# A two-layer transformer and state-space block: the scan with all five engines in written order, diagonal matmuls, and its last preparation moved

## The chip, the cores and the metric

The kernel runs on one core of one Trainium2 chip. The metric is the device time of one execution in microseconds (us), as the median of several runs. Engines are named as the profile names them: PE (TensorE matmuls and transposes) with PEld (its weight loads), DVE (VectorE), ACT (ScalarE), POOL (GpSimd) and SP (SyncE, which issues most DMAs). A name with a q, such as SPq or ACTq, is the engine's sequencer. Everything is float32.

## The reference

The input x has 4 sequences of 512 tokens with 512 channels. Layer 0 adds an attention, then a gated feed-forward network (FFN) with weights quantised to three values. Layer 1 adds a selective scan, and then an attention over small latents with a mixture of experts (top 2 of 7 and a shared one). The scan is what matters here:

```python
xz = einsum('btd,rd->btr', x, W_xproj)          # x here is the layer norm, "u"
delta_r, B_mat, C_mat = xz[..., :128], xz[..., 128:144], xz[..., 144:]
delta = softplus(einsum('btr,dr->btd', delta_r, W_dt) + b_dt)
dA = exp(delta[..., None] * -exp(A_log))        # 16 states per channel
Bu = delta[..., None] * B_mat[:, :, None, :] * x[..., None]
h_t = dA_t * h_{t-1} + Bu_t;  y_t = sum over n of h_t * C_t
return y + x * D_param
```

## The kernel before, in words

The four sequences (b = 0 to 3) lie in SBUF as xs[b], tokens on partitions in four tiles t of 128. The stages follow one another: attention of layer 0, FFN, scan, latent attention, router, experts.

**FFN** (lines 594 to 715). For each b, 11 hidden tiles f: `gated` makes 16 matmuls into a pair of PSUM banks (L651, high and low parts of the input, hTh and hTl), ACT takes the silu (L656), DVE the product (L657) and the parts gh and gl, and `down` (L669) adds the tile into four banks one tile later. PE's order is written by hand (`manual_schedule`, L674); the other engines are ordered by a scheduler. Between the matmuls the generator `prepare(b - 1)` (L495) is advanced by `part`: three parts per tile, with some left out at the first two tiles. It makes the inputs of the scan for the sequence whose FFN is done:

- statistics (L107), normalised rows row_s (L122), x += u D on POOL (L508, L509), and uT, the transposed u (L131, L132);
- delta_r as drT (L520, L524), the latents B and C by four matmuls of 512 columns (L529), copied to bcT; C goes to DRAM as c_rows (L536), B is transposed into bts (L540, L543), one column per token tile and state;
- per channel tile k: z by a matmul (L551), |z| on ACT (L552, into the buffer e), max(z, 0) on DVE (L553, into delta); exp(-|z|) on ACT (L555); a correction u = e - ((e + 1) - 1) added to delta by three DVE operations on SBUF (L559 to L561); log(1 + e) (L563) added on DVE (L568). That is the softplus;
- delta to DRAM (L569), delta times u on DVE (L571), transposed (L576), copied (L578) and stored as dxs (L579).

The preparation of b = 3 does not fit behind any FFN tile and runs inside the scan.

**Scan** (lines 815 to 966). The work is 128 steps (b, n, half): 16 states n for each sequence, and two halves of the channel tiles. Only PE is in written order. Before the loop come `fetch(0)` (L894: two loads of 1 MB, delta_l and dxT, L828 and L830) and seven pieces of `prepare(3)` (L900 to L904). At the first half of each state, `scale` of the next state makes on ACT four copies bu of dxT scaled by B (L839) and four exponentials da (L845). In each step PE transposes bu into two banks for the step after (`turn`, L853), DVE runs two scans over time (`scan`, L861), POOL multiplies h by the broadcast C (`weigh`, L872, the load cb at L869 is on SP), and PE adds hc, transposed, into four banks of sums for the step two back (`add_up`, L885; hc has three buffers). After a sequence's last step DVE adds the sums to x (L892). The loads of sequence b + 1 go out at state 3 of sequence b (L912). Further pieces of `prepare(3)` run in odd steps, what is left in step 56 (L923); then pools change hands, and the weights of the latent attention are loaded. From step 76 `enter(0)` (L725), the first preparation of that attention, is advanced in every third step: statistics, normalised h on DVE (L735), squares on ACT (L739), rows on DVE (L749), transposes (L753), latents (L760).

Of the kernel before, what the change touches and what calls it, by code (L numbers as in the profile page):

```python
# [19 lines left out]
P = 128  # L20
# [10 lines left out]
NS = 16  # L31
# [15 lines left out]
def block_kernel(ctx: ExitStack, tc: tile.TileContext, a: dict, out: bass.AP):  # L47
# [46 lines left out]
    dxs = tc.dram_tile([B * T, C], F32, name="dxs")  # L94

# [40 lines left out]
    def project_back(srcT, w, x):  # L136

        for t in range(NT):
            y = bank("y")
            for k in range(NK):  # L140
                nc.tensor.matmul(
                    y, srcT[:, k, t * P : (t + 1) * P], w[:, k, :], start=k == 0, stop=k == NK - 1
                )
            nc.vector.tensor_tensor(x[:, t, :], x[:, t, :], y, ALU.add)

# [337 lines left out]

    def scan_constants(pool):
# [4 lines left out]
        for k in range(NK):  # L489
            diag = pool.tile([P, P], F32, tag="diag", name="diag")  # L490
            nc.vector.tensor_scalar(diag, ident, dcol[:, k : k + 1], None, ALU.mult)
            nc.tensor.matmul(dp[:, k * P : (k + 1) * P], ones, diag, start=True, stop=True)
        nc.scalar.copy(dpar, dp)

    def prepare(b, pool, spot, ahead):  # L495
# [30 lines left out]

        pb = spot("pb")
        for k in range(NK):
            nc.tensor.matmul(  # L529
                pb[: 2 * NS, :], wx[:, k, RANK:], uT[:, k, :], start=k == 0, stop=k == NK - 1  # L530
            )
            if k == 1:
                yield
        bcT = pool.tile([2 * NS, T], F32, tag="bcT", name="bcT")
        nc.scalar.copy(bcT, pb[: 2 * NS, :])
        nc.sync.dma_start(c_rows[b], bcT[NS:, :])  # L536
        yield
        pb = spot("pbt")
        for t in range(NT):
            nc.tensor.transpose(  # L540
                pb[:, t * NS : (t + 1) * NS], bcT[:NS, t * P : (t + 1) * P], ident[:NS, :NS]
            )
        nc.scalar.copy(bts[:, b, :], pb[:, : NT * NS])  # L543
# [45 lines left out]

    def half_pair(name):  # L590
        return pair(name)[:, 0, :]


    with tc.tile_pool(name="b_s", bufs=1) as bs, tc.tile_pool(name="b_1", bufs=1) as b1, tc.tile_pool(
# [16 lines left out]
        def inputs(b, mv=None):  # L611

            high = b2.tile([P, NK, T], F32R, tag="hTh", name="hTh")
            low = b2.tile([P, NK, T], F32R, tag="hTl", name="hTl")
# [59 lines left out]
        with tc.manual_schedule(engines={mybir.EngineType.PE}):  # L674
# [4 lines left out]
            for b in range(B):  # L679
# [14 lines left out]
                for f, rows in enumerate(FROWS):  # L694
# [5 lines left out]
                    part(3 * f + 1)  # L700
                    if b == 0 and f == 4:
                        scan_constants(b2)
# [22 lines left out]
    def enter(b, pool):  # L725

        mv = pool.tile([P, NT, 2], F32, tag="mv", name="mv_d")
        for t in range(NT):
# [3 lines left out]
            yield  # L732
        ss = pool.tile([P, NT], F32, tag="ss", name="ss_d")
        for t in range(NT):
            nc.vector.tensor_scalar(  # L735
                hs[b][:, t, :], xs[b][:, t, :], mv[:, t, 0:1], rs[:, t : t + 1], ALU.subtract, ALU.mult
            )
# [6 lines left out]
        before = None  # L744
        for t in range(NT + 1):
            row = None
            if t < NT:
                row = pool.tile([P, C], F32, tag="row", name="row_d", bufs=2)
                nc.vector.scalar_tensor_tensor(  # L749
                    row, hs[b][:, t, :], rs[:, t : t + 1], ln1, ALU.mult, ALU.mult  # L750
                )
            if before is not None:
# [63 lines left out]
    with tc.tile_pool(name="c_f", bufs=2, reuse_waits="tile") as cf, tc.tile_pool(  # L816
        name="c_1", bufs=1
    ) as c1, tc.tile_pool(name="c_2", bufs=2) as c2:

        das = [c1.tile([P, NK, T], F32, tag=f"da{i}", name=f"da{i}") for i in range(2)]  # L820
        for da in das:
            nc.vector.memset(da[:, :, 0:1], 0.0)
        steps = [(b, n, half) for b in range(B) for n in range(NS) for half in range(2)]
        loaded, scaled, decays, turned, states, weighed, sums = {}, {}, {}, {}, {}, {}, {}

        def fetch(b):
            delta = cf.tile([P, NK, T], F32, tag="delta_l", name="delta_l")
            nc.sync.dma_start(delta, by_rows(deltas[b]))  # L828
            dxT = cf.tile([P, NT, C], F32, tag="dxT", name="dxT")
            nc.sync.dma_start(dxT, by_tokens(dxs, b))  # L830
            loaded[b] = delta, dxT

        def scale(b, n):

            delta, dxT = loaded[b]
            rows = []
            for t in range(NT):
# [10 lines left out]
        def turn(b, n, half):  # L848
            bu = [bank("bu") for _ in range(2)]
            for i in range(2):  # L850
                k = 2 * half + i
                for t in range(NT):
                    nc.tensor.transpose(  # L853
                        bu[i][:, t * P : (t + 1) * P], scaled[b, n][t][:, k * P : (k + 1) * P], ident
                    )
            turned[b, n, half] = bu
# [9 lines left out]
        def weigh(b, n, half):  # L866
# [4 lines left out]
            hc = c2.tile([P, 2, T], F32, tag="hc", name="hc", bufs=3)  # L871
# [5 lines left out]
        def add_up(b, n, half):  # L877
# [12 lines left out]
            if n == NS - 1 and half == 1:  # L890
                for t in range(NT):
                    nc.vector.tensor_tensor(xs[b][:, t, :], xs[b][:, t, :], sums[b][t], ALU.add)  # L892

        fetch(0)  # L894
        last = ExitStack()
        cp = last.enter_context(tc.tile_pool(name="c_p", bufs=1, side="right", reuse_waits="tile"))
        between = prepare(B - 1, cp, bank, 4)
        come = enter(0, c1)
        with tc.manual_schedule(engines={mybir.EngineType.PE}):
            for _ in range(2):  # L900
                next(between)
            scale(0, 0)
            for _ in range(5):
                next(between)  # L904
            turn(*steps[0])
            for m, (b, n, half) in enumerate(steps):
                if half == 0:
# [4 lines left out]
                    if n == 3 and b + 1 < B:  # L912
                        fetch(b + 1)
# [599 lines left out]
```

## Time and profile before

| what | us |
|---|---|
| median of 3 runs (1941.34 to 1942.9) | 1942.84 |
| profiled execution | 1946.77 |
| its span | 1945.0 |
| attention of layer 0 | 0 to 432 |
| FFN | 432 to 753 |
| scan, with the last preparation | 753 to 1122 |
| entry of the latent attention | 1122 to 1157 |
| latent attention | 1157 to 1575 |
| router, experts | 1575 to 1945 |

Busy over the span: PE 1764.7 us (91%), DVE 1145.5, ACT 948.2, POOL 580.9. In the stretch 763 to 1118: PE 286.1, DVE 332.0, ACT 326.6, POOL 311.1 of 355.

How to read the lines below. A group's line gives line, engine, operation, out<-in with partitions x elements, the count, then busy us and mean ns of one, then the engine's idle time just before them and what ended most of it. A line of the timeline gives start and length in us, engine, line, operation, and in brackets the idle time before it with its releaser. A windows line gives the window, its length, then busy us and instruction count of PE, PEld, DVE, ACT and POOL, the granted clock of PE as a share of full speed, the DMA share and GB/s.

### The profile page before, as it was taken

The page shows a single profiled execution, that of the slowest core. Times are in us where ns is not written, and L with a number is a line of the kernel's source. Part 1 is how long each engine was busy: PE and PEld are TensorE (multiplying, and loading weights), DVE is VectorE, ACT ScalarE, POOL GpSimd, SP SyncE. Part 2 cuts the span into 40 slices and gives each one's busy share as a digit, 9 for nine tenths or more (in the row PEclk, how much of TensorE's full clock was granted, in tenths as well). Part 3 has the DMA queues.
Part 4 walks back from the last instruction along what each step waited for, and adds up shares of the span by engine and source line. Part 5 has one row for each costly group of instructions (what it writes and reads, how often), then busy time and mean ns, then how long its engine had stood idle before and what let it go on. Part 6 is the DMA issues. An engine that isn't in the chain of part 4 may idle for free. (4 is left out here: it accounts for less than half of the span.)

```text
span 1945.0 us, 26741 instructions
## 1 busy us (share of the span) xinstructions
PE 1764.7 (91%) x9970; PEld 1060.5 (55%) x9970; DVE 1145.5 (59%) x1849; ACT 948.2 (49%) x1945; POOL 580.9 (30%) x391
## 2 busy tenths in 40 slices
PE   7999999989999897967887889999999988999997
PEld 3433343337666665766776645555555544545443
DVE  6456435666454646999998865564655734322223
ACT  2434433332242436978999836665665732111110
POOL 2221212110202014867998910101000000244430
PEclk9999999999999998989999978999999999999998
DMA  7003200111010104123411100010001006255546
GB/s 245 8 1 99 69 1 1 44 30 47 1 39 7 44 1 152 54 100 89 143 56 46 43 1 1 1 44 1 33 23 38 29 11 235 74 93 91 91 72 190
DMA packets 70884, 114.24 MB, mean 59 GB/s; under 512 B 7962, under 2 KB 26778, under 8 KB 70756
## 3 DMA queue, kind: packets, MB, share of 16 engines
q1 hardware_dynamic: 59796, 88.02, 14.1%
q0 software_dynamic: 8656, 20.32, 5.9%
q10 hardware_dynamic: 2304, 4.20, 0.6%
q8 instruction: 80, 1.31, 0.3%
q14 instruction: 48, 0.39, 0.1%
HBM read 81.18 MB, written 31.33 MB: 58 GB/s over the span
## 5 line engine op out<-in xcount | busy, mean ns | idle before, releaser
L872 POOL TENSOR_TENSOR hc<-h,cb 128x1024 f32<-128x1024 f32 x128 | 303.2, 2410 | 43.3 <-DVE h L861 20.9
L861 DVE TENSOR_TENSOR_SCAN h<-da,bu 128x512 f32<-128x512 f32 x256 | 289.7, 1197 | 15.0 <-ACT da L845 6.9
L853 PE MATMUL bu<-ident,bu 128*128 128x128 f32 x1024 | 165.0, 290 | 55.5 <-DVE h L861 32.7
L271 PE MATMUL pq<-wqkv,hT 128*128 128x512 f32 x384 | 181.2, 620 | 0.7 <-ACT hT L132 0.7
L853 PEld LDWEIGHTS bu<-ident,bu 128*128 128x128 f32 x1024 | 121.7, 147 | 88.6 <-ACT bu L839 49.3
L845 ACT ACTIVATE da<-delta_l,am 128x511 f32<-128x511 f32 x256 | 165.9, 739 | 4.2 <-DVE h L861 4.2
L839 ACT ACTIVATE bu<-dxT,bts 128x512 f32<-128x512 f32 x256 | 165.7, 738 | 0.0
L1101 ACT ACTIVATE pr<-scd,nm 128x128 f32<-128x128 f32 (+3 forms) x256 | 133.1, 528 | 56.3 <-DVE nm L1098 53.6
L651 PE MATMUL pg<-hTh,w 128*128 128x512 f32 (+1 forms) x352 | 148.7, 422 | 9.3 <-DVE sil L657 8.0
L885 PE MATMUL ys<-ident,hc 128*128 128x128 f32 x1024 | 143.4, 285 | 13.4 <-POOL hc L872 11.2
L651 PE MATMUL pg<-hTl,w 128*128 128x512 f32 (+1 forms) x352 | 140.7, 400 | 0.2 <-DVE hTl L639 0.2
L1400 PE MATMUL pgr<-wgu,gTe 128*128 x304 | 137.1, 593 | 0.0
L885 PEld LDWEIGHTS ys<-ident,hc 128*128 128x128 f32 x1024 | 121.6, 147 | 21.7 <-POOL hc L872 18.0
L351 ACT ACTIVATE pt<-sc 128x1024 f32<-128x1024 f32 (+3 forms) x128 | 84.2, 698 | 84.2 <-PE sc L346 81.7
L271 PEld LDWEIGHTS pq<-wqkv,hT 128*128 128x128 f32 x384 | 72.1, 196 | 94.6 <-issue 86.3
L1090 PE MATMUL scd<-qkTd 32*128 32x512 f32 (+3 forms) x512 | 108.3, 504 | 12.9 <-ACT pr L1101 11.9
L102 POOL TENSOR_TENSOR ri_ln<-ri_ln,minus_half 128x4 f32<-128x4 f32 (+1 forms) x17 | 16.9, 994 | 302.6 <-DVE ri_ln L101 298.4
L1098 DVE TENSOR_REDUCE nm<-scd 128x2 f32<-128x256 f32 (+3 forms) x128 | 104.2, 815 | 0.0
L1113 PEld LDWEIGHTS tpd<-ident,pr 128*128 128x128 f32 x640 | 70.4, 145 | 61.0 <-issue 41.5
L1113 PE MATMUL tpd<-ident,pr 128*128 128x128 f32 x640 | 102.2, 292 | 0.6 <-ACT pr L1101 0.6
L352 POOL TENSOR_SCALAR_AFFINE_SELECT pt<-pt 128x512 f32<-128x512 f32 x64 | 43.5, 679 | 196.2 <-ACT pt L351 196.2
L1093 DVE TENSOR_TENSOR scd<-scd,neg 128x256 f32<-128x256 f32 x128 | 54.9, 430 | 69.8 <-PE scd L1090 67.7
(260 smaller groups left out, 3109.1 us busy)
## 6 DMA issues: line engine op xcount, KB each, us to landing
cb<-c_rows SPq DMA_DIRECT2D x64, 256.0 KB, 3.2
q_w<-in_w2T SPq DMA_DIRECT2D x20, 256.0 KB, 2.8
deltas<-delta SPq DMA_DIRECT2D x16, 256.0 KB, 2.1
dxs<-st SPq DMA_DIRECT2D x16, 256.0 KB, 2.5
delta_l<-deltas SPq DMA_DIRECT2D x4, 1024.0 KB, 9.0
dxT<-dxs SPq DMA_DIRECT2D x4, 1024.0 KB, 7.1
acc<-h SPq DMA_DIRECT2D x16, 256.0 KB, 2.0
hrows<-h SPq DMA_DIRECT2D x4, 1024.0 KB, 4.3
```

What stands on the lines that cost most here:

```text
L271: nc.tensor.matmul(y, inputs_T[b][:, k, t * P : (t + 1) * P], wqkv[:, k, s * C : (s + 1) * C], start=k == 0, stop=k == NK - 1,)
L651: nc.tensor.matmul(pg[:rows, i, :], w[:, k, f * P : f * P + rows], part[:, k, :], start=k + m == 0, stop=k + m == NK,)
L839: nc.scalar.activation(row, dxT[:, t, :], AF.Copy, scale=bts[:, b, t * NS + n : t * NS + n + 1])
L845: nc.scalar.activation(da[:, k, 1:], delta[:, k, 1:], AF.Exp, scale=am[:, k, n : n + 1])
L853: nc.tensor.transpose(bu[i][:, t * P : (t + 1) * P], scaled[b, n][t][:, k * P : (k + 1) * P], ident)
L861: nc.vector.tensor_tensor_scan(h[:, i, :], decays[b, n][:, 2 * half + i, :], bu, 0.0, ALU.mult, ALU.add)
L872: nc.gpsimd.tensor_tensor(hc, states.pop((b, n, half)), weighed[b, n].unsqueeze(1).to_broadcast([P, 2, T]), ALU.mult)
L885: nc.tensor.matmul(sums[b][t][:, k * P : (k + 1) * P], hc[:, i, t * P : (t + 1) * P], ident, is_transpose=True, start=n == 0 and k == 0, s ...
L1090: nc.tensor.matmul(sc[:, i, :w], qkT[at, g, t * P : w], qkT[at, NG + g, :w], start=True, stop=True)
L1101: nc.scalar.activation(pr[:, i, :w], sc[:, i, :w], AF.Exp, bias=nm[:, i : i + 1], accum_out=sums[b, g][:, t, 2 * p + i : 2 * p + i + 1],)
L1113: nc.tensor.transpose(tp[:, j * P : (j + 1) * P], pr[:, i, j * P : (j + 1) * P], ident)
L1400: nc.tensor.matmul(pg, gT[:, k, :], wgu[:, bass.ds(e, 1), k, :].rearrange("p e o -> p (e o)"), start=k == 0, stop=k == NK - 1,)
```

## The change

All line numbers in this section are those of before.

- **Order.** In the scan all five engines (PE, DVE, ACT, POOL, SP) run in written order. A step issues: batch-end additions (`finish`, now three steps into the next sequence), a piece of the last preparation, a piece of `enter(0)`, `scale`, the first bank of the next `turn`, the scans, the product, `add_up` of the step three back (hc has four buffers), and the second bank of the next `turn`.
- **Diagonals.** For token tile 0 the scaled copy of dxT and its transposes are replaced by a matmul of dxT with a diagonal matrix of B, which SP loads from DRAM (64 KB per state). ACT makes three copies per state. The diagonals of all 16 states are made when the sequence is prepared: one DVE product of 128x2048, and a store of 1 MB to `diags`, from SP in the FFN and from ACT in the scan. In the FFN the product is written to the buffer e, which |z| overwrites next.
- **Latents.** 16 matmuls of 128 columns, which put the token tiles side by side on the partitions, and one transpose replace four matmuls of 512 columns and four small transposes; C is stored in four parts. The preparation has one piece fewer there.
- **Last preparation** (`prepare_last`). Rows by ACT (scale and shift) in place of DVE; e + 1 and - 1 by ACT; the four terms of the softplus (max(z, 0), e, minus ((e + 1) - 1), logarithm) are summed by PE into a bank, with the identity and its negative as weights; u D is a product with diagonals on PE, added by DVE. Its DMAs go out on ACT. Three pieces come in steps 0 to 2, then one in each odd step from 5, the rest in step 84.
- **Loads.** `fetch(b)` goes out in quarters. The buffers are shared with hTh and hTl of the FFN, so that `fetch(0)` goes out at the start of the FFN's last sequence; those of b = 1 and 2 in four steps of the sequence before, that of b = 3 in steps 84 to 87. The weights of the latent attention are loaded one per step from step 88.
- **`enter`.** Shifted h and rows on ACT instead of DVE, for every b. The weight ln1 is multiplied into the two weight matrices by eight POOL operations in steps 100 to 106, instead of into the rows. The 14 pieces of `enter(0)` run from step 86 to 125.

The diff, cut to its core:

```diff
+    def shift_of(pool, mv, rs):
+        shift = pool.tile([P, NT], F32, tag="shift", name="shift")
+        nc.vector.scalar_tensor_tensor(shift, mv[:, :, 0], -1.0, rs, ALU.mult, ALU.mult)
+        return shift
+
+    def shifted(dst, x, t, rs, shift):
+        nc.scalar.activation(
+            dst, x[:, t, :], AF.Identity, bias=shift[:, t : t + 1], scale=rs[:, t : t + 1]
+        )
...
+    large = scans.enter_context(tc.tile_pool(name="large", bufs=2, reuse_waits="tile"))
+    def fetch(b):
+        delta = large.tile([P, NK, T], F32, tag="one", name="delta_l")
+        dxT = large.tile([P, NT, C], F32, tag="two", name="dxT")
+        loaded[b] = delta, dxT
+        for i in range(NT):
+            nc.sync.dma_start(dxT[:, i, :], by_tokens(dxs, b)[:, i, :])
+            nc.sync.dma_start(delta[:, i, :], by_rows(deltas[b])[:, i, :])
+            yield
...
+    def latents(pb, uT):
+        for k in range(NK):
+            for t in range(NT):
+                nc.tensor.matmul(
+                    pb[t * 2 * NS : (t + 1) * 2 * NS, :P], wx[:, k, RANK:], uT[:, k, t * P : (t + 1) * P],
+                    start=k == 0, stop=k == NK - 1,
+                )
...
+    def keep_inputs(b, pb, room):
+        nc.scalar.copy(
+            bts[:, b, :].rearrange("p (t n) -> p t n", t=NT),
+            pb[:, :P].rearrange("p (t n) -> p t n", t=NT)[:, :, :NS],
+        )
+        diag = room.rearrange("p k t -> p (k t)").rearrange("p (n q) -> p n q", n=NS)
+        nc.vector.tensor_tensor(
+            diag, ident.unsqueeze(1).to_broadcast([P, NS, P]),
+            bts[:, b, :NS].unsqueeze(2).to_broadcast([P, NS, P]), ALU.mult,
+        )
+        return diag
...
     def prepare(b, pool, spot, ahead):
...
+        keep_latents(b, bcT, nc.sync)
         yield
         pb = spot("pbt")
+        nc.tensor.transpose(pb[:, :P], bcT, ident)
+        e = pool.tile([P, NK, T], F32, tag="e", name="diag_s")
+        nc.sync.dma_start(diags[b], keep_inputs(b, pb, e))
         yield
...
+    def prepare_last(b, pool):
...
+        diag = keep_inputs(b, pb, pool.tile([P, NK, T], F32, tag="ln", name="diag_s"))
+        relu = pool.tile([P, NK, T], F32, tag="relu", name="relu")
+        for k in range(NK + 1):
+            if k > 0:
+                nc.scalar.activation(e[:, k - 1, :], pz, AF.Abs, bias=bdt[:, k - 1 : k])
+                nc.vector.tensor_scalar(relu[:, k - 1, :], pz, bdt[:, k - 1 : k], 0.0, ALU.add, ALU.max)
+            if k < NK:
+                pz = bank("pz")
+                nc.tensor.matmul(pz, wdt[:, k * P : (k + 1) * P], drT, start=True, stop=True)
+            if k == NK // 2:
+                nc.scalar.dma_start(diags[b], diag)
+            yield
+        over = pool.tile([P, NK, T], F32, tag="over", name="over")
+        for k in range(NK):
+            nc.scalar.activation(e[:, k, :], e[:, k, :], AF.Exp, scale=-1.0)
+            if k % 2 == 1:
+                yield
+        for k in range(NK):
+            nc.scalar.activation(over[:, k, :], e[:, k, :], AF.Identity, bias=ones[:, 0:1])
+            nc.scalar.activation(over[:, k, :], over[:, k, :], AF.Identity, bias=minus_one)
+            yield
+        ln = pool.tile([P, NK, T], F32, tag="ln", name="ln")
+        nc.scalar.activation(ln, e, AF.Ln, bias=1.0)
+        yield
...
+        terms = ((ident, relu), (ident, e), (minus, over), (ident, ln))
...
+                for i, (w, term) in enumerate(terms):
+                    nc.tensor.matmul(pd, w, term[:, k, :], start=i == 0, stop=i == 3)
...
         def scale(b, n):
             delta, dxT = loaded[b]
-            rows = []
-            for t in range(NT):
+            diag = c1.tile([P, P], F32, tag="diag", name="diag_l", bufs=3)
+            nc.sync.dma_start(diag, diags[b][:, n, :])
+            rows = [diag]
+            for t in range(1, NT):
...
+        def turn(b, n, half, i):
+            bu = bank("bu")
+            k = 2 * half + i
+            nc.tensor.matmul(
+                bu[:, :P], loaded[b][1][:, 0, k * P : (k + 1) * P], scaled[b, n][0],
+                start=True, stop=True,
+            )
+            for t in range(1, NT):
+                nc.tensor.transpose(
+                    bu[:, t * P : (t + 1) * P], scaled[b, n][t][:, k * P : (k + 1) * P], ident
+                )
...
+        engines = {getattr(mybir.EngineType, e) for e in ("PE", "DVE", "Activation", "Pool", "SP")}
+        with tc.manual_schedule(engines=engines):
             scale(0, 0)
-            for _ in range(5):
-                next(between)
-            turn(*steps[0])
+            turn(*steps[0], 0)
+            turn(*steps[0], 1)
             for m, (b, n, half) in enumerate(steps):
+                if m % each == 3 and b > 0:
+                    finish(b - 1)
+                if m >= 5 and m % 2 == 1:
+                    next(between, None)
+                if m >= 86 and m % 3 == 2 and m < 86 + 3 * 14:
+                    next(come)
...
                 if m + 1 < len(steps):
-                    turn(*steps[m + 1])
+                    turn(*steps[m + 1], 0)
                 scan(b, n, half)
                 weigh(b, n, half)
-                if m >= 2:
-                    add_up(*steps[m - 2])
+                if m < 3:
+                    next(between, None)
+                if m >= 3:
+                    add_up(*steps[m - 3])
+                if m + 1 < len(steps):
+                    turn(*steps[m + 1], 1)
-                if m == 56:
+                if m == 84:
...
+            for step in steps[-3:]:
                 add_up(*step)
+            finish(B - 1)
```

## The prediction

> **What bounds the kernel now.** I read the profile page first, then windows by stage, then the scan's own groups, waits and timeline. Two stages are touched, the gated FFN (432 to 753 us from the span's start) and the scan (753 to 1122); the attention before and the stages after 1157 keep their code. The windows show what limits each (columns: window, length, busy us and count of PE, PE weight loads, DVE, ACT, POOL, then the granted PE clock, DMA share, GB/s):
>
> ```profile
> 432.00:753.00 321.00, 304.25 (x1292) 224.58 (x1292) 173.00 (x279) 119.15 (x168) 40.05 (x30) 0.99 0.11 35
> 795.00:870.00 75.00, 55.66 (x375) 47.59 (x374) 74.28 (x68) 70.48 (x108) 54.79 (x24) 0.90 0.25 85
> 955.00:980.00 25.00, 22.00 (x169) 17.93 (x168) 25.00 (x25) 25.00 (x42) 24.66 (x12) 1.00 0.36 128
> ```
>
> The FFN is TensorE's: 304 of 321 us. In the scan's quiet part (955 to 980) DVE, ACT and POOL are all full. While the last preparation runs (795 to 870) DVE is full, ACT nearly, and POOL has fallen to 73%. The groups of the scan:
>
> ```profile
> L872 POOL TENSOR_TENSOR hc<-h,cb 128x1024 f32<-128x1024 f32 x128 | 303.2, 2410 | 43.3 <-DVE h L861 20.9
> L861 DVE TENSOR_TENSOR_SCAN h<-da,bu 128x512 f32<-128x512 f32 x256 | 289.7, 1197 | 15.0 <-ACT da L845 6.9
> ...
> L845 ACT ACTIVATE da<-delta_l,am 128x511 f32<-128x511 f32 x256 | 165.9, 739 | 4.2 <-DVE h L861 4.2
> L839 ACT ACTIVATE bu<-dxT,bts 128x512 f32<-128x512 f32 x256 | 165.7, 738 | 0.0
> ```
>
> In the quiet part the starts of consecutive products on POOL are 2.335 us apart, scans on DVE 1.11 (2.22 a step), exponentials and copies on ACT 0.613, and transposes 0.109, sixteen a step (1.75). Two steps of one state n so cost POOL 4.67, DVE 4.44, ACT 8 x 0.613 = 4.91 and PE 3.5. From the first scan (762.6) to the end of the last product (1117.9) the stage takes 355.3 us; in 763 to 1118 DVE is busy 332.0, ACT 326.6, POOL 311.1. So none is full, and the 7% over the fullest is lost where DVE is held up and the others follow. The timeline shows how: L560 there takes 2.74 us, and a PE wait stands behind it:
>
> ```profile
> 832.97 2.74 DVE L560 TENSOR_TENSOR u<-e,u 128x512 f32<-128x512 f32 x1
> ...
> 837.68 0.72 PEld L853 LDWEIGHTS bu<-ident,bu 128*128 128x128 f32 x4 [4.08 <-ACT bu L839]
> ...
> 841.86 2.74 DVE L561 TENSOR_TENSOR delta<-delta,u 128x512 f32<-128x512 f32 x1
> ```
>
> The same shapes beside an idle POOL took 0.67 to 0.7 us. In this stage L560 averages 1.72 and L568 1.42, and L735 of the next stage's entry reaches 2.59; DVE operations that read PSUM beside the same POOL (L553, L892) stay at 0.66 to 0.75. Steps with such work last 5.4 to 8.8 us in place of 2.3 (steps 21, 23, 25, 31, 47, 49, 101).
>
> **1. The start of the scan.** PE idles 6.31 us (750.94 to 757.65) for DVE's row_s, and the first scan starts at 762.6. The old order puts seven pieces of preparation and both 1 MB loads (issued 752.7 and 753.2) ahead of it. The new one loads batch 0 in quarters during the FFN's last batch, and the first steps need only 3 copies and an exponential: from about 749.3, 3 x 0.61 + 1.28 (table load, L845's row) + 0.61 gives 753; the FFN's last addition on DVE ends at 752.7. First scan about 753.3: **-9.3 us**, bounds -6 (the clock was 0.5 from 752 for 10.24 us, which doubles the first transposes, and the two clears of da go first) and -12.
>
> **2. The scan.** Per state ACT does 3 copies instead of 4, so 7 x 0.613 = 4.29: under POOL's 4.67. The last preparation costs ACT: rows 4 x 0.61, transposes out 4 x 0.49, drT 0.59, bcT 0.25, Abs 4 x 0.69, exponentials 4 x 0.61, eight identities x 0.61, logarithm 1.92 with two table loads of 1.28, eight copies x 0.59, thirteen DMA issues at most x 0.34 (L1451 issues from ACT at 0.338), and the entry of the next stage 10.3: 40 us together. DVE's extras: eight statistics x 0.72, one 128x2048 product 2.29 (L1332's row), relu 4 x 0.66, twelve batch-end additions and four of D u at 0.6, four products with uT x 0.66: 24. POOL: three powers x 1.0 and eight 128x256 scalings x 0.5: 7. Sums: ACT 64 x 4.29 - 4.3 (the last state copies nothing ahead) + 40.2 = 310.5; DVE 128 x 2.22 + 23.9 = 308.3; POOL 128 x 2.335 + 7 = 305.9. PE stays under 2.3 a step. Lower end: the largest sum, 311, if buffers absorb every piece. Upper end: the sum over the 64 states of the dearest engine in each, 345. Today's stage is 1.07 of its fullest engine; 1.07 x 311 = 332, and as the stretched DVE operations that make today's excess leave, and adding up three steps behind with four hc buffers gives PE one step more, I take 330. **-25.3 us** (bounds -44 to -10).
>
> What could replace the removed copy: row 0 of bu now comes from a matmul with a diagonal that SP loads (64 KB per state). cb of 256 KB lands in 3.2 us median and the new load is issued a state ahead (4.67 us), so it costs nothing unless SP's issue is late; uncovered it would hold PE by about 3 us at that state. A diagonal matmul is f32 with 128 columns. The f32 matmuls of L271, 512 columns, start 0.429 us apart at full clock: 0.107 per 128, the same as a transpose, so PE keeps 1.75 a step.
>
> The Trainium skill (FP8 and Floating Point Precision, TensorE Precision Notes) speaks against this part: true FP32 takes four passes through the array. If a transpose were one pass and the matmul four, two of the sixteen would cost 0.33 more each, 2.40 a step, and PE would pass POOL for 8 us more in 128 steps. L271's row does not show that excess over transposes, and I go by the row.
>
> All five engines are now in written order, so a late operand stops what is queued behind it: an ACT piece waiting for a preparation matmul holds the next state's copies and exponentials, and through da the scan. That is in the distance from 311 to 345. After PE gaps of 2.84 us (at 554) and 6.31 us (at 757) the rows show a granted clock of 0.5 in windows of 3.41 and 10.24 us; 16 transposes then take 3.5 a step, over POOL's 2.335. The quiet part ran at 1.00 with almost nothing but transposes, so I put this in the upper end.
>
> **3. The FFN.** Batches 1 to 3 of it prepare scan inputs between matmuls. PE's order is by hand, so what a piece waits for is PE's stall. Removed per piece set: four latents matmuls (1.72) become sixteen small ones (4 x 0.11): -1.3. Added: a 128x2048 product on DVE (2.29) and a 1 MB store from the buffer that Abs writes next. So bts copy, product 2.29, issue 0.4, store, Abs 0.69, relu 0.75, and only then the second pz's pair of banks is free; PE waits there, and behind Abs on ACT stand the silu and the high part of the next FFN tile. A 1 MB store SBUF to DRAM in this kernel (hrows<-h) lands after 4.3 us median. The second pz would then start 5.8 us later than the matmul before it would let it, and an idle window of that length lowers the clock for 3.41 us, +1.7. One piece fewer moves the later pieces up by one part, which shortens a PE wait of 3.1 us there and its half clock (clock 0.5 from 553.98 for 3.41 us) by 3.5. So 5.8 + 1.7 - 1.3 - 3.5 = +2.7 for b = 1, 2, and 4.5 + 1.7 - 1.3 = +4.9 for b = 3, where other parts are used: **+10**. Lower end -7, the store hidden and only the gains left. Upper end +43, if the store takes 15.3 us, as the 1 MB x<-in_x loads do (three times 11 more).
>
> **4. After the scan.** The next stage's entries get 12 to 16 us of ACT for what DVE did. They lie in 1122 to 1157, where ACT is busy 12.6 of 35 us and PE 30.3, and later beside attention, where PE is busy 392 of 418: +2 (bounds -1 to +7). The weight loads spread from step 88 to the end on SP leave ahead of their first use but for the last two; nothing.
>
> Sum: -9.3 - 25.3 + 10 + 2 = -22.6. The profiled execution took 1946.77 us (span 1945.0), 3.9 over the median of the three runs, 1942.84. So 1924.2 profiled, **1920 us** as a median.
>
> **Rivals.** *A, the engines pack:* the stage runs at its largest sum, 312 instead of 330 (-18), and the store hides in part (0 to -12): 1890 to 1908. For it: POOL already runs back to back through 25 steps. Against: 345 of the unbuffered sum. *B, pieces stall the written orders:* 345 (+15) with the FFN as forecast: 1935, to 1939 with a further half-clock window. For it: every piece lands on one state and ACT's logarithm (4.5 us in one) exceeds the buffers' lead of about one state. *C, slower:* the store of the diagonals. PE has no other work ahead of the second pz; at the 15.3 us of the 1 MB loads the FFN gives back 43, not 10: 1953. It decides from a landing of 4.3 + 22.6/3 = 11.8 us. For: the 1 MB loads x<-in_x and wqkv at 15.3 and 10.1 us. Against: those came in the crowded first 60 us, this one meets a DMA share of 0.11. *D, no change:* B and half of C together, 1939 to 1947. That the code does not do what it says is excluded by the instruction order: ACT has 3 copies and 4 exponentials per state, PE 1 matmul and 3 transposes per bank.
>
> **Chances.** Forecast (1908 to 1935) 0.5; A 0.2; B 0.15; D 0.06; C 0.09. 0.2% of 1942.84 is 3.9 us, about what a measurement of this kernel can tell from no change. Faster 0.85, same 0.06, slower 0.09. The range leaves out C, D's upper half and A's lower end: 1895 to 1941.
>
> **What would show it.** Step 1: a first scan between 752 and 756. Step 2: 320 to 340 us from first scan to last product, no DVE operation of the stage over 1.2 us but the product and batch ends, no step over 4.5. Step 3: a PE wait of about 6 us before the second pz of each prepared batch, ended by Abs. Step 4: pl of the first entry 4 us after the last product, as now. I am wrong if products on POOL are over 2.4 us apart in quiet steps, if PE's clock stays under 0.9 in the scan, or if the store's landing is over 8 us.

## The result, and the profile after

The changed kernel takes the same time: 1943.08 us median (1939.54 to 1949.36, 12 runs) against 1942.88 for the kernel before in the same rounds, ratio 1.0003, 95% interval 0.999 to 1.0015. The forecast was 1920. Its profiled execution took 1941.63 us (span 1939.9). Single executions of either kernel differ by up to 10 us, so I compare stages of the profiles, not single times.

| stage, us | before | after | step of the prediction |
|---|---|---|---|
| FFN, first to last matmul | 318.9 | 321.3 | +10 |
| from there to the first scan | 11.3 | 3.0 | -9.3 |
| first scan to the end of the last product | 355.3 | 359.2 | -25.3 |
| from there to the latent attention's first scores | 38.9 | 37.6 | +2 |
| the rest | 788.3 | 785.6 | 0 |

The same windows of the changed kernel (window, length, then busy us of PE, PEld, DVE, ACT, POOL, clock, DMA share, GB/s):

```profile
432.00:753.00 321.00, 294.95 (x1354) 223.11 (x1355) 176.96 (x277) 119.47 (x170) 40.41 (x30) 0.98 0.15 49
795.00:870.00 75.00, 67.98 (x550) 60.58 (x549) 67.71 (x63) 65.55 (x108) 62.81 (x27) 0.98 0.32 101
955.00:980.00 25.00, 24.58 (x174) 19.79 (x173) 21.63 (x20) 21.42 (x36) 20.59 (x9) 1.00 0.37 104
```

In the second window POOL has gone from 54.8 to 62.8 us: the old bad stretch is better. In the third it has gone from 24.7 to 20.6: the stretch that was full is now full of holes. The page's groups of the scan (the copies are 192 instead of 256):

```profile
L1038 POOL TENSOR_TENSOR hc<-h,cb 128x1024 f32<-128x1024 f32 x128 | 300.9, 2387 | 109.3 <-DVE h L1027 90.4
L1027 DVE TENSOR_TENSOR_SCAN h<-da,bu 128x512 f32<-128x512 f32 x256 | 291.4, 1199 | 26.4 <-PE bu L1019 13.3
...
L1007 ACT ACTIVATE da<-delta_l,am 128x511 f32<-128x511 f32 x256 | 163.9, 709 | 6.1 <-DVE h L1027 6.1
...
L1001 ACT ACTIVATE bu<-dxT,bts 128x512 f32<-128x512 f32 x192 | 124.2, 711 | 24.3 <-PE bu L1019 22.5
```

POOL's idle 109.3 contains the wait of 67.9 us ahead of the first product; 41.4 lie inside the scan. ACT now waits 22.5 us for PE: its spare time is not used.

The best reading is by step: the distance between starts of successive products on POOL, less the quiet 2.335 us. The excess of all 128 steps is 57.9 us after and 50.3 before (where, besides, the first product comes 6.1 us after the first scan, now 2.4). In the changed kernel the quiet steps are as forecast (2.31 to 2.35 us in steps 6 to 16, 39 to 52 and 108 to 125); the excess sits in few places:

| steps | excess, us | what stands there |
|---|---|---|
| 85 | 6.5 | diag_l and cb late on SP |
| 84 | 3.7 | the clearing of wr on POOL, which waits for a store to land |
| 34, 66, 98 | 8.1 | batch-end additions on DVE, and a piece |
| 100, 102, 104, 106 | 8.3 | scalings by ln1 on POOL, the second power |
| 17, 30 | 7.1 | instructions that wait at the head of a line; the product of the diagonals |
| 55 | 4.2 | logarithm on ACT with two table loads |
| 0 to 2 | 4.0 | statistics between the first scans |
| 72, 78 | 3.7 | ux, which waits for ACT's copy of delta |
| 94 | 2.4 | 128x4 operation on DVE |
| others | 10.0 | up to 0.7 each, relu, additions of u D, statistics |

The two largest together, steps 84 and 85, in the timeline of the changed kernel (start, length, engine, line, in brackets the idle time and its releaser):

```profile
994.29 0.33 SPq L1106 DMA_DIRECT2D ln<-in_ln_w  x1
...
994.37 0.20 POOL L1109 MEMSET wr<- 128x128 f32 x1 [3.55 <-DMA dxs<-st]
...
997.60 0.43 SPq L997 DMA_DIRECT2D diag_l<-diags  x1
998.08 0.43 SPq L1035 DMA_DIRECT2D cb<-c_rows  x1
...
1002.73 0.77 PE L1014 MATMUL bu<-diag_l,dxT 128*128 128x128 f32 x2 [7.82 <-DMA diag_l<-diags]
...
1003.37 4.67 POOL L1038 TENSOR_TENSOR hc<-h,cb 128x1024 f32<-128x1024 f32 x2 [6.48 <-DMA cb<-c_rows]
```

The load of ln2 and the clearing of wr (the router's weights) take memory of the last preparation, whose store of dxs must land first. POOL stands 3.55 us at the clearing, with a product behind it (step 84). SP is in written order too, so diag_l and cb, which the next steps need, stand behind the load of ln2 and behind four of the eight loads for b = 3 (step 85). At step 30 the same happens on DVE, for 2.83 us and then the 2.29 of the product:

```profile
839.39 0.19 ACT L533 COPY bts<-pbt 128x64 f32<-128x64 f32 x1
839.49 1.95 ACT L1001 ACTIVATE bu<-dxT,bts 128x512 f32<-128x512 f32 x3
839.62 2.29 DVE L538 TENSOR_TENSOR diag_s<-ident,bts 128x2048 f32<-128x2048 f32 x1 [2.83 <-ACT bts L533]
...
844.29 2.37 POOL L1038 TENSOR_TENSOR hc<-h,cb 128x1024 f32<-128x1024 f32 x1 [4.55 <-DVE h L1027]
```

In the FFN the forecast wait is there, for b = 1 and 2:

```profile
538.03 0.69 ACT L603 ACTIVATE e<-pz,bdt 128x512 f32<-128x512 f32 x1 [5.54 <-DMA diags<-diag_s]
538.75 0.75 DVE L604 TENSOR_SCALAR delta<-pz,bdt 128x512 f32<-128x512 f32 x1 [4.11 <-ACT e L603]
539.55 1.22 PE L602 MATMUL pz<-drT,wdt 128*128 128x512 f32 x1 [4.59 <-DVE delta L604]
```

### The profile page after: what moved, and what is told of

It is laid out like the page before. It is cut to its first block, busy times and chain, and to the rows that moved or that the text cites. A ratio compares the mean times of both kernels' runs of the same rounds, so it can differ in the third digit from the quotient of the medians.

```text
span 1939.9 us, 27518 instructions
## 1 busy us (share of the span) xinstructions
PE 1778.6 (92%) x10374; PEld 1096.5 (57%) x10374; DVE 1119.0 (58%) x1812; ACT 938.5 (48%) x1932; POOL 574.7 (30%) x391
## 5 line engine op out<-in xcount | busy, mean ns | idle before, releaser
L1038 POOL TENSOR_TENSOR hc<-h,cb 128x1024 f32<-128x1024 f32 x128 | 300.9, 2387 | 109.3 <-DVE h L1027 90.4
L1019 PE MATMUL bu<-ident,bu 128*128 128x128 f32 x768 | 134.5, 283 | 7.0 <-ACT bu L1001 6.9
L1001 ACT ACTIVATE bu<-dxT,bts 128x512 f32<-128x512 f32 x192 | 124.2, 711 | 24.3 <-PE bu L1019 22.5
L1014 PE MATMUL bu<-diag_l,dxT 128*128 128x128 f32 x512 | 109.0, 296 | 26.8 <-DVE h L1027 15.0
L1014 PEld LDWEIGHTS bu<-diag_l,dxT 128*128 128x128 f32 x512 | 82.0, 199 | 47.1 <-DVE h L1027 26.3
L1019 PEld LDWEIGHTS bu<-ident,bu 128*128 128x128 f32 x768 | 97.6, 147 | 11.0 <-ACT bu L1001 10.9
```

The costliest lines, as they stand in the source:

```text
L1001: nc.scalar.activation(row, dxT[:, t, :], AF.Copy, scale=bts[:, b, t * NS + n : t * NS + n + 1])
L1014: nc.tensor.matmul(bu[:, :P], loaded[b][1][:, 0, k * P : (k + 1) * P], scaled[b, n][0], start=True, stop=True,)
L1019: nc.tensor.transpose(bu[:, t * P : (t + 1) * P], scaled[b, n][t][:, k * P : (k + 1) * P], ident)
L1038: nc.gpsimd.tensor_tensor(hc, states.pop((b, n, half)), weighed[b, n].unsqueeze(1).to_broadcast([P, 2, T]), ALU.mult)
```

## The experiments

All are edits of the changed kernel. Ratios are to the kernel before on the same chip. The theories on trial: **no slack**, POOL, DVE and ACT are so equally loaded that an inserted piece costs its whole length; **order**, what costs is instructions that aren't ready and hold ready ones behind them; and against the first, that the engines take the pieces back (the packing that my 330 us rested on).

**1. SP cleared.**

```diff
-                    nc.sync.dma_start(ln2, a["ln2_w"].partition_broadcast(P))
...
-                    nc.gpsimd.memset(wr, 0.0)
...
+                    hold(ln2, a["ln2_w"].partition_broadcast(P))
+                    hold(wr[:, :, :NR], by_rows(a["router_w"]))
+                    hold(br, a["router_b"].partition_broadcast(P))
+                if m == 91:
+                    nc.gpsimd.memset(wr, 0.0)
-                if m >= 84:
+                if m >= 87:
                     next(coming, None)
-                if m >= 88 and loads:
+                if m >= 91 and loads:
```

> The changed kernel with the loads of ln2, wr and br put behind the weight loads, the clearing of wr at step 91, and the loads for b = 3 from step 87 instead of 84, so that nothing on SP waits for the buffers of the last preparation. Queue theory: steps 84 and 85 lose 10.2 us because diag_l and cb stand on SP behind loads that wait for those buffers; they go back to about 2.4 us each and the time falls by 8 to 11 us, to about 1933. Rival, traffic: the eight 256 KB loads for b = 3 crowd out diag_l and cb wherever they stand; the wait moves with them and the time falls by 0 to 4 us.

Ratio 0.9981 (0.9971 to 0.9991). The scan takes 351.1 us, 8.1 less; steps 84 and 85 have an excess of 1.8 and 0.7 instead of 3.7 and 6.5. The loads of diag_l and cb that stood in line (997.60 and 998.08) now go out 16 us earlier:

```profile
981.68 0.32 SPq L997 DMA_DIRECT2D diag_l<-diags  x1
...
982.09 0.38 SPq L1035 DMA_DIRECT2D cb<-c_rows  x1
...
990.87 2.39 POOL L1038 TENSOR_TENSOR hc<-h,cb 128x1024 f32<-128x1024 f32 x1 [1.80 <-DVE h L1027]
```

For step 85 the queue theory holds: the traffic is the same and costs nothing three steps later. The 1.9 us at step 84 are not SP's: there POOL no longer stands 3.55 us at the clearing of wr, which this run moves as well. The time fell by 4 us only against the changed kernel (0.9981 against 1.0003), about half of what the scan gained and short of the 8 to 11 expected; no run shows where the rest went.

**2. Scalings on DVE.**

```diff
-                        nc.gpsimd.tensor_scalar(w, w, ln1[:, k : k + 1], None, ALU.mult)
+                        nc.vector.tensor_scalar(w, w, ln1[:, k : k + 1], None, ALU.mult)
```

> The changed kernel with the eight scalings of the weights by ln1 on DVE instead of POOL. No-slack theory (every piece on POOL or DVE costs its own length, since POOL, DVE and ACT stand within 10% of each other): POOL loses 8 x 0.92 = 7.4 us, DVE gains 8 x 0.3 to 0.45, so the time falls by 3.5 to 5 us. Rival, order (what costs is waiting in a written line, short pieces are covered): within 1.5 us of the changed kernel.

Both missed: ratio 1.0029 (1.0016 to 1.0042), the scan 2.6 us longer. The groups of this run in 1030 to 1075 say why (busy, mean ns):

```profile
L1149 DVE TENSOR_SCALAR w_b<-w_b,ln 128x256 f32<-128x256 f32 x4 | 9.8, 2451 | 0.0
L1149 DVE TENSOR_SCALAR wlat<-wlat,ln 128x256 f32<-128x256 f32 x4 | 2.4, 607 | 0.0
```

Of two equal operations in a row the second takes four times as long: it starts with one of POOL's products, and lasts its 2.4 us.

**3. Only PE in written order.**

```diff
-        engines = {getattr(mybir.EngineType, e) for e in ("PE", "DVE", "Activation", "Pool", "SP")}
+        engines = {mybir.EngineType.PE}
```

> The changed kernel with only PE in written order, as before; the scheduler orders DVE, ACT, POOL and SP. Order theory: the waits in line go away (2.2 us at step 17, 2.8 at 30, 4.3 at 55, 10 at 84 and 85), the scan takes 335 to 345 us instead of 359, the time is 1920 to 1930. No-slack theory: the pieces stay, the scan takes 350 to 362, the time is 1935 to 1947.

Ratio 0.9976 (0.9966 to 0.9986). The scan takes 348.0 us, 11.2 less, and so falls between the two. Steps 84 and 85 have no excess, 30 and 55 lose 1.1 and 2.3, 17 keeps its 2.5 (that wait is PE's, which is still by hand), the four scalings' steps have none; but 36 to 41, where the scheduler drew the statistics of `enter(0)` forward, have 6.2 (0.9 in the changed kernel) and 90 and 91 have 8.0 (0.5), where it put the eight scalings ahead of two products, the first of them behind a load of weights. Of the 11.2 us by which the full written order is dearer here, run 1 gets back 8.1 with the order kept. The time fell by 5 us against the changed kernel, again about half.

**4. Two steps behind.**

```diff
-            hc = c2.tile([P, 2, T], F32, tag="hc", name="hc", bufs=4)
+            hc = c2.tile([P, 2, T], F32, tag="hc", name="hc", bufs=3)
...
-                if m >= 3:
-                    add_up(*steps[m - 3])
+                if m >= 2:
+                    add_up(*steps[m - 2])
```

> The changed kernel with sums added up two steps behind and three buffers hc, as before. Order theory: PE meets products that are not ready and holds the next transposes, 3 to 8 us slower. No-slack theory: PE has 0.5 us to spare in a step, within 1.5 us of the changed kernel.

The scan takes 360.9 us, 1.7 more, all at step 66 (4.8 instead of 2.9 over). Adding up three behind is worth 1.7 us. The ratio, 1.0028 (1.0015 to 1.0041), is 5 us above that of the changed kernel, more than this explains; outside the scan the two profiles differ by 5.3 us, in stages that were not edited.

**5. Uses one piece later.** Besides the lines below, the copy of bts and the product of the diagonals are two pieces.

```diff
                 yield
+        yield
         pd = bank("pd")
...
-                if m >= 5 and m % 2 == 1:
+                if m in (3, 4) or m >= 5 and m % 2 == 1:
```

> The changed kernel with three places of the last preparation moved apart: the matmuls on uT, and the product of the diagonals on DVE, come one piece after the ACT copies that they need, and two more pieces are taken at steps 3 and 4. Order theory (an instruction that is not ready holds ready ones behind it on its engine): the 2.5 us over the usual step at step 17 and 2.3 of the 4.6 at step 30 go, the scan is 4 to 5 us shorter than the 359.2 of the changed kernel. No-slack theory (only the length of the pieces counts): within 1 us of 359.2.

Steps 17 and 30 are 2.5 and 2.3 us shorter, as the order theory has it. But the two pieces that I drew forward to make room cost 2.5 at step 2, so the scan is only 2.6 shorter and the time is that of before (0.9997, 0.9985 to 1.0009).

**6. No batch-end additions.**

```diff
-                if m % each == 3 and b > 0:
-                    finish(b - 1)
```

> The changed kernel without the additions of the sums to x for b = 0, 1, 2 (left out, so x lacks the scan's output there; the DVE work falls by 12 x 0.67 = 8.1 us). No-slack theory: each such piece costs its own length, the steps 34, 66 and 98 fall from 5.3, 5.2 and 4.6 us to 2.4 to 2.8, the scan is 7 to 8.5 us shorter. Rival, lead: the engines take back what a short piece costs within a few steps, the scan is 0 to 3 us shorter.

The scan is 5.4 us shorter (353.8), between the two expectations. Steps 34 and 98 are 2.5 and 2.3 shorter, about the whole length of four additions; step 66 keeps 2.8. There, first in the changed kernel and then in this run:

```profile
937.05 2.46 DVE L1059 TENSOR_TENSOR x<-x,ys 128x512 f32<-128x512 f32 x4
```

```profile
941.16 0.69 DVE L735 TENSOR_TENSOR ux<-pdl,uT 128x512 f32<-128x512 f32 x1 [2.16 <-ACT delta L732]
```

ux, which had stood behind the additions without a wait, now waits 2.16 us for ACT's copy of delta. No slack, then: where nothing else is late, a piece of 2.46 us costs 2.3 to 2.5. The time was 0.9994 (0.998 to 1.0008), with an FFN of 326.1 us in this profile; the eight profiles with the same FFN code and order, the changed kernel's among them, lie between 320.7 and 326.1.

**7. No diagonals.** Run 4 is its counterpart.

```diff
-            rows = [diag]
-            for t in range(1, NT):
+            rows = []
+            for t in range(NT):
...
-        nc.sync.dma_start(diags[b], keep_inputs(b, pb, e))
+        keep_inputs(b, pb)
```

> The changed kernel without the diagonals (four copies per state on ACT, eight transposes a step, no product, store or load of diagonals) and with sums added up two steps behind and three hc buffers, to be set beside the run that has only the latter (358.5 us from first product to last). If ACT bounds: 8 x 0.613 = 4.91 us per state against POOL's 4.67, the quiet steps go from 2.335 to 2.45, and with the preparation on ACT the scan is 12 to 18 us longer, less 2.3 at step 30. Rival, catching up: ACT gains on the others while they stand at pieces of their own, the scan is 2 to 6 us longer. The FFN loses the two waits of 4.59 us for the store, and is 2 to 6 us shorter.

This is the run that settles the balance. The scan takes 373.1 us, 12.2 more than run 4: ACT bounds, as forecast, though the 12 us come in lumps (4.1 of them at step 17, 2.6 at step 49) and most steps stay near 2.34. And the FFN takes 308.7, 12.0 or more below every one of those eight. The two windows of this run:

```profile
432.00:741.00 309.00, 293.48 (x1355) 222.93 (x1355) 170.44 (x276) 119.51 (x171) 39.71 (x30) 0.99 0.14 42
743.00:1117.00 374.00, 304.03 (x2199) 257.12 (x2197) 315.34 (x301) 346.42 (x566) 311.17 (x142) 0.94 0.24 73
```

ACT is busy 346 of 374 us there. So the diagonals give the scan 12 us and take the same 12 from the FFN (ratio of this run 1.0, 0.9987 to 1.0012).

**8. Three mended.** Runs 1 and 5 together, and

```diff
-                        nc.gpsimd.tensor_scalar(w, w, ln1[:, k : k + 1], None, ALU.mult)
+                    nc.scalar.activation(w, w, AF.Copy, scale=ln1[:, k : k + 1])
```

> The changed kernel with three things mended at once: the loads that stood on SP moved behind the weight loads (8.1 us by the profile of that run alone), the two uses moved one piece later (4 to 5), and the scalings by ln1 on ACT, one a step from 98, instead of POOL (7.3 on POOL; 8 x 0.4 on ACT, which has 0.38 us a state to spare there). If the costs add up: 8.1 + 4.5 + 4 to 7, a scan of 340 to 343 us, and a time 12 to 18 us under the kernel before. If ACT becomes the bound from step 98: 345 to 350 us, 6 to 12 under it.

Ratio 0.9956 (0.9943 to 0.9969), a scan of 347.8. Runs 1 and 5 add up (8.1 + 2.6); the scalings gain 0.8. On ACT they take away the excess of 5.5 at steps 100 to 104 and leave 1.6 and 6.0 at 105 and 106 (none and 2.8 before), where DVE stands 5.89 us for ACT's square. ACT has no room there either.

**9. Diagonals by DMA.** The matrices are zeroed once; the view `diagonals` has a stride of one row and one element.

```diff
-        nc.sync.dma_start(diags[b], keep_inputs(b, pb, e))
+        keep_inputs(b, pb)
+        nc.sync.dma_start(diagonals(b), bts[:, b, :NS])
```

> The changed kernel, its diagonals made without the product of 128x2048 and without the 1 MB store: the matrices are set to zero in DRAM once, ahead of the FFN (4 DMAs of 1 MB), and per sequence one DMA writes the 2048 diagonal elements straight from bts. The scan's matmuls with diagonals stay. Theory: making the diagonals costs the FFN what the run without diagonals showed, 12.5 us, by the two waits of 4.59 us, the 1.6 and the half clock behind them; the FFN takes 308 to 310 us instead of 321, step 30 of the scan loses 2.3 us, the time is 12 to 15 us under the kernel before. Rival: the FFN's gain in the run without diagonals came from elsewhere (other order of the scheduler's engines): the FFN takes 317 to 321 us, the time is 0 to 5 under.

Ratio 0.9962 (0.9947 to 0.9976). The two waits are gone and sequences 1 and 2 take 79.0 and 82.9 us in the FFN against 86.7 and 88.1. The small DMA lands no sooner than the 1 MB store did (3.9 us median, both); what is gone is that |z| must wait for a buffer that is still being stored. A buffer of its own for the product might do the same; that was not tried. In the scan the 4.6 at step 30 go and 3.0 come at step 32. But sequence 0 takes 75.6 instead of 64.9, where the zeros run beside the loads of the weights, and the FFN as a whole 318.6, the rival's range without the rival's reason:

```profile
448.37 0.80 PE L812 MATMUL pg<-hTh,w 128*128 128x512 f32 x1 [7.76 <-DVE sil L818]
```

**10. No eps on DVE.**

The new helper's two operations; it stands in for `root_inverse` in `prepare_last` and `enter`.

```diff
...
+        nc.gpsimd.tensor_scalar(r, v, eps, None, ALU.add)
+        nc.gpsimd.tensor_tensor(r, r, minus_half[:, : v.shape[1]], ALU.pow)
...
```

> The changed kernel with the addition of eps ahead of each power on POOL instead of DVE in the last preparation and the entry (the factor 1/C goes into the squares on ACT). In the changed kernel's trace the 128x4 DVE operations of L102 take 1.92 and 3.72 us beside POOL's products, 0.14 beside an idle POOL. Port theory: DVE is held until POOL's product ends, and scans stand behind it; without these the steps 94 and 106 are 1 to 2.5 us shorter each, though POOL has 3 short operations more: scan 2 to 4 us shorter. Rival: the DVE operations waited for their inputs and the scans would wait anyway: scan 0 to 3 us longer, by POOL's new operations of about 1 us.

The rival has the number: scan 359.8 (+0.6), ratio 1.0004 (0.9991 to 1.0017). Step 94 is 1.1 shorter, as the port theory has it, but step 106 is 0.4 longer: there DVE's scans wait for POOL, which does the work now. Step 17 is 1.7 longer for a reason that is neither's: PE's clock is 0.5 there for 3.41 us, and two matmuls take 2.01 us instead of 1.13. Nor did the long operations all go; the next 128x4 one on DVE, shift, got longer. First the groups of the changed kernel, then of this run:

```profile
L102 DVE TENSOR_SCALAR ri_rms<-ss_d 128x4 f32<-128x4 f32 x1 | 3.7, 3715 | 2.7 <-ACT sq_d L900 2.7
L102 DVE TENSOR_SCALAR ri_ln<-mv_d 128x4 f32<-128x4 f32 x1 | 1.9, 1915 | 0.0
L150 DVE SCALAR_TENSOR_TENSOR shift<-mv,ri_ln 128x4 f32<-128x4 f32 x1 | 1.3, 1333 | 0.0
L150 DVE SCALAR_TENSOR_TENSOR shift<-mv_d,ri_ln 128x4 f32<-128x4 f32 x1 | 0.5, 479 | 0.0
```

```profile
L156 DVE SCALAR_TENSOR_TENSOR shift<-mv,ri_ln 128x4 f32<-128x4 f32 x1 | 1.8, 1783 | 0.0
L156 DVE SCALAR_TENSOR_TENSOR shift<-mv_d,ri_ln 128x4 f32<-128x4 f32 x1 | 1.3, 1307 | 0.0
```

The timelines give the reason. The second shift ends at 1033.07 in the changed kernel, where a product of POOL ends at 1033.06, and at 1034.53 in this run, where one ends at 1034.52; the first ends 0.02 us after a product in both. How long such an operation takes depends on how much of POOL's product is left when it starts.

**11. All mended.** Runs 1, 5 (without drawing pieces forward), 9 and 10, and the scalings at steps where POOL stands anyway:

```diff
+                if m in (98, 106, 127):
```

> The changed kernel with five things mended: the loads on SP behind the weight loads (8.1 us measured), the two uses one piece later (2.5 and 2.3 us measured), the scalings put at steps where POOL stands anyway, 98, 106 and after the last product (5 to 7 of 8.2 us), diagonals by DMA (12.5 in the FFN, 2.3 in the scan), eps on POOL (2 to 4). If they add up: a scan of 333 to 339 us from first scan to last product, an FFN of 308 to 310, a time of 1908 to 1916. If mending one only shows the next wait: a scan of 343 to 350, a time of 1920 to 1930.

Ratio 0.986 (0.984 to 0.9881), 1917.86 us. The scan takes 341.1, 2 us above the range for costs that add up: they nearly do, and steps 100 to 104 have no excess now. The FFN, 318.4, still has the zeros of run 9.

**12. Zeros later.**

```diff
+                    if b == 1 and f == 0:
+                        nc.vector.tensor_scalar(minus, xs[0][:, NT - 1, :P], 0.0, None, ALU.mult)
+                        for z in range(B):
+                            nc.gpsimd.dma_start(matrices(z), minus.unsqueeze(1).to_broadcast([P, NS, P]))
```

> The kernel with all five things mended, and the matrices set to zero in DRAM after the FFN's first sequence instead of at the FFN's start (the zeros are made from x of sequence 0, so that their DMAs can't go out sooner). In the run before, the loads of the quantised weights stood beside the four 1 MB DMAs of zeros, PE waited 7.76 us at 448 and had half its clock for 10.24 us; the first FFN sequence took 75.6 us against 64.9. Theory: that is all due to the zeros' traffic; the FFN takes 308 to 310 us, 9 to 11 less, and the time falls to about 1907 to 1910. Rival: the traffic only moves, and delays the first preparation's stores and loads by as much: 1914 to 1920.

1907.59 us (1904.1 to 1910.42), ratio **0.981** (0.9795 to 0.9824): faster than both kernels. The time is where the theory put it; the FFN takes 305.7 us, a little under its 308, its first sequence 65.1 instead of 75.7 in run 11, and the scan 341.9:

```profile
432.00:743.00 311.00, 294.61 (x1376) 224.02 (x1377) 176.74 (x284) 124.22 (x176) 44.34 (x34) 1.00 0.19 55
742.00:1085.00 343.00, 314.64 (x2458) 279.25 (x2457) 314.54 (x298) 308.41 (x501) 308.95 (x142) 0.98 0.32 94
```

## Why the prediction was wrong, by its steps

**Step 1, the start: right.** 8.3 of the forecast 9.3 us. About 4 of it is given back at once, because the pieces that stood ahead of the scan now stand in its first steps.

**Step 2, the scan: this is where it failed.** The term was 330 us, "1.07 x 311", the largest engine sum and a little. Measured: 359.2. The engine sums themselves were near (DVE busy 319.9, ACT 308.3 and POOL 311.6 in 757 to 1117, against 308, 310 and 306; the first two were summed 1 us too high, as their terms add up to 307 and 309.5), and so was the diagonals' share. What was wrong is that they pack. A step gives DVE a lead of 2.335 - 2.22 = 0.115 us over POOL, so a piece of 2.46 us needs 21 quiet steps to be paid for ahead, and pieces come every second step. Run 6 shows it at steps 34 and 98. The upper end of my bounds, the sum over states of the dearest engine, 345, was the nearer number, and still 14 too low. With runs 1 and 5 the gap closes: 359.2 - 8.1 (step 84's clearing and SP) - 4.8 (waits in line at 17 and 30) = 346.3. That agreement is partly luck, since the POOL scalings took 0.92 us each and not 0.5, and the 128x4 operations on DVE, 1.3 to 3.7 us beside POOL, had no term. Even run 11, with all of this mended, stays at 341.1, 30 above the largest sum.

The term at nothing failed too: the new load of diag_l "costs nothing unless SP's issue is late", about 3 us at a state if it is, and then no term. I looked at when the loads were needed, not at what stands on SP behind loads that must wait for memory; those of ln2, wr and br in step 84, and the clearing of wr, are nowhere in the sum. Run 1 puts the late loads at 5.8 us and the clearing at 1.9, 8.1 for the scan.

My 1.07 came from the kernel before, whose excess I put down to DVE operations stretched beside POOL. Those did leave (128x512 operations of DVE take 0.66 to 0.73 us in the scan now), but an excess of the same size came from other places. I take it for a property of the balance rather than of those operations; no run on the kernel before shows that.

**Step 3, the FFN: mechanism right, size smaller.** Forecast +10, measured +2.4 by one profile of each. The wait for the store is there (4.59 us, forecast 5.8) for b = 1 and 2; for b = 3 the scheduler put a silu ahead and PE waited 1.6. Run 7 splits the sum: the preparation without the diagonals makes the FFN 10.2 us shorter than before (the gains in my sum add up to 10.9, though I wrote 7 as the lower end), making them costs 12.6 (21.2 in my sum). Most of the difference is b = 3, 6.2 us in the sum: with the diagonals its sequence takes 81.6 us, without them 81.0.

**Step 4: small, as forecast,** but with the other sign: +2 forecast, -1.3 measured (37.3 to 39.6 in all profiles of these runs, 38.9 before).

**Rivals.** B, pieces that stall the written orders, was the case, but priced at 1935 to 1939 without step 84's loads. D has the number, 1939 to 1947, by chance: it needs half of C, and C did not come, as the 1 MB store landed after 3.9 us. Nor did any of the three signs of being wrong show: quiet products stand 2.335 us apart, PE's clock in the scan is 0.95, and the landing is under 8 us. They watched the prices of the steps, not what waits between them.

On the f32 matmuls the row was the right guide. The Trainium skill (FP8 and Floating Point Precision, TensorE Precision Notes) gives true FP32 four passes. In this trace two f32 matmuls with a diagonal take 0.39 us and three f32 transposes 0.49, about 0.1 more for each further one of either kind (one matmul 0.28, eight transposes 1.04): no excess over transposes.

Not settled: the ratios of runs 2 and 4 are higher than their scans explain, those of runs 1 and 3 fell by half of what their scans gained, and single profiles of one FFN differ by 5 us, twice the +2.4 of step 3.

## What to carry to other kernels

When several engines stand within a few per cent of each other, forecast inserted work by the dearest engine in each short stretch, not by totals: a lead of 0.1 us a step pays for little. For each engine put into written order, ask of every instruction, DMA issues above all, what it waits for and what is ready behind it. And charge a saving in one stage with what its inputs cost in the stage that makes them: here 12 us saved by the diagonals had been spent on making them, and one DMA of 8 KB in place of a product and a 1 MB store, with the zeros at a quiet time, was worth about as much as the rest: the FFN of run 12 is 15.6 us shorter than the changed kernel's, its scan 17.3.

## What the runs showed of the hardware

- A DVE operation of 128x4 took 0.14 us beside an idle POOL and 1.3, 1.9 and 3.7 us beside POOL's products, each ending 0.02 to 0.04 us after a product; the longest spans the end of one product and the whole of the next. Of two equal operations of 128x256 one took 0.53 and the other 2.45. The size of the operation does not protect it. The Trainium skill (SBUF - State Buffer, "SBUF: two separate sides") describes a port pair that a GpSimd operation, or a VectorE operation in a 2-port mode or with two SBUF inputs, holds for the whole instruction while the other engine is blocked; that fits these rows; whether those of one input ran in such a mode, no run shows. In run 10, with the additions of eps gone from DVE, the next such operation there still fell beside a product, and took 1.31 us instead of 0.48.
- A DMA of 2048 single elements of 4 bytes, from SBUF to strided places in DRAM, landed after 3.9 us median in run 9 and 4.2 in run 12, about as late as a 1 MB store of whole rows (3.9).
- Four 1 MB stores from a 64 KB tile of zeros landed after 12.4 us median beside weight loads, which came late, and PE stood 7.76 us (run 9); issued after the FFN's first sequence they landed after 8.9, and no such wait shows (run 12).
